# Moving four stages of a software pipeline within its period: a four-layer convolution network on one core

## The chip, the cores and the metric

The kernel runs on one core of a Trainium2 chip. The metric is the device time of one execution in microseconds (us). A core has TensorE (PE, with its weight loads shown as PEld), VectorE (DVE), ScalarE (ACT), GpSimd (POOL) and SyncE (SP, which here only issues DMAs). Each engine works through its own list of instructions, and semaphores order them between engines.

## The reference

The input x is 16 images of 64 x 64 pixels with 256 channels in float32. Four layers follow each other; each adds its result to x, and each works on a group norm (32 groups, over pixels and the group's channels) of its input:

- Layer 0: for each pixel the nearest of 1024 code vectors is found, and that vector is the result: `argmin(|x|^2 + |e|^2 - 2 x.e)`, then a gather.
- Layer 1: attention within each row of 64 pixels, `f = x Wf + bf`, `g = x Wg + bg`, `h = x Wh + bh`, `sigmoid(f g^T) h`.
- Layer 2: three projections of each pixel to a number, x0, x1 and x2. For every pair of the 4096 pixels n, m of an image `sim = x0[n] * x1[m]`, a softmax over n, `feats[m] = sum over n of x2[n] * softmax`, and the result is `sigmoid(feats[m]) * x`. These are 4096 x 4096 exponentials per image.
- Layer 3: linear attention with 4 heads of 32: softmax of q over the head's channels and of k over the pixels, a context matrix k v^T, its product with q, an output projection and a layer norm.

All arithmetic that matters for time is in float32.

## The kernel before

**Tiling.** A batch is one image: 4096 tokens, in 8 chunks of 512 tokens (4 tiles of 128). A chunk with its 256 channels on 2 x 128 partitions is a tile of 512 KB, and between stages it goes to DRAM and back. Each layer is cut into stages, and each stage is a Python generator that issues some instructions and then yields a number, the plan's measure of what it has issued:

- `stats0` (L287) loads a batch and takes its group-norm statistics.
- `search`, `stage1` (L303), is layer 0: the distances in `pd` (L377), VectorE's maximum (L384) and index search (L389) per tile of 128 tokens, 32 tiles per batch, the gather through POOL (L390).
- `layer1` (L416): `attend` and `mix` per chunk; `ph` and `po` are its large products, its result is added in L511. Search and layer 1 share two wide PSUM buffers (`wide`, L71).
- `rows`, `rows2` (L540): loads the 8 chunks again (`xr`), computes x0, x1, x2 in `pr` (L565), brings them to DRAM and, transposed, to `x01` (L575). `spread_rows` (L582) loads one row of 2048 numbers to all partitions.
- `exps`, `stage2` (L592): layer 2's exponentials, 64 pairs per batch of an exponential on ScalarE (L617) and a product with sum on VectorE (L620). The exponent's offset `nmax` comes from the extremes of x0 over all pixels (L598 to L604), which needs a reduction over partitions on POOL (L601). Its `nmax` tile has one buffer.
- `gate`, `gate2` (L653): per chunk the gate's row is loaded to all partitions (`gb`, L667), ScalarE makes `u` from it twice (L674), VectorE multiplies (L675) and takes statistics, and the chunk is stored (L681). `gb` has one buffer, `u2` two.
- `layer3`, `stage3` (L689): a first pass over the chunks for keys, queries, values and the context (L731 to L791), and a second for the output (`form`, `variance`, `po`, `pxo`, `y`).

**Order.** The instructions are traced in the order of a plan at the end of the kernel. Its unit is a period: the search of batch b lies at b to b + 1. `task` (L880) gives every stage of every batch a start, not before its predecessor's end plus a lag and not before the same stage of the batch before has ended, and a length. A heap then takes the generator that is next in plan time, lets it issue until its next yield, and moves it on by `length * step / total`. So the plan sets no time on the chip; it sets which instruction stands before which in each engine's list and in each queue. Work under `high_priority` may go ahead of it, and a DMA whose buffer is free may be issued ahead of an earlier one that waits. Six or so stages of as many batches lie in one period, in the steady part each once:

| stage of batch | search b | stats0 b+1 | layer1 b-1 | rows b-1 | exps b-2 | gate b-2 | layer3 b-3 |
|---|---|---|---|---|---|---|---|
| plan, from the period's start | 0 to 1 | 0.30 to 0.80 | 0.06 to 0.76 | 0.79 to 0.89 | -0.07 to 0.93 | 0.99 to 1.79 | -0.17 to 0.83 |

(The gate that starts at 0.99 runs into the next period, as do exps and layer 3. The gate and layer 3 have fewer units than their `total`, so that their last yields lie at some 0.88 of their lengths.) The first batches have a shorter layer 1 and the last ones shorter stages, by the constants of L33 to L38 and the lines of the loop (L886 to L898). In the last batch the exponentials are made in 8 parts, with the gate's chunks behind them.

Of the kernel before, what the change touches and what calls it, by code (L numbers as in the profile page):

```python
# [9 lines left out]
F32 = mybir.dt.float32  # L10
# [3 lines left out]
ALU = mybir.AluOpType  # L14
AX = mybir.AxisListType
# [14 lines left out]
HEADS = 4  # L30
DH = 32
URGENT = 3000
LAG1, LEN1 = 0.06, 0.7  # L33
LAGR = 0.03
LAG2 = 0.17
LAG3, LENG = 0.06, 0.8
LAG4 = 0.04
LEN3 = {0: 0.4, 1: 0.33, 2: 0.37}  # L38

# [2 lines left out]
def kernel(  # L42
# [497 lines left out]
    def rows2(b):  # L540
        tag = f"r2_{b}"
        scale, nmean, _ = norm2[b]
        with tc.high_priority(offset=URGENT):
            pb = bank(f"pbr_{tag}")
            for k in range(NK):
                nc.scalar.activation(
                    wrow_n[:, k, :].rearrange("p (j n) -> p j n", n=32)[:, :, 0:3],
                    wrow_raw[:, k : k + 1, 0:3].to_broadcast([P, 4, 3]), AF.Copy, scale=scale[:, k : k + 1],
                )
            for k in range(NK):  # L550
                nc.tensor.matmul(
                    pb[:, 0:1], lhsT=wrow_n[:, k, :], rhs=nmean[:, k : k + 1], start=(k == 0), stop=(k == NK - 1)
                )
            brow_n = small.tile([P, 1], F32, tag="brow_n", name=f"brow_{tag}")
            nc.scalar.activation(brow_n, pb[:, 0:1], AF.Identity, bias=brow)
        x01 = small.tile([P, NT, 2], F32, tag="x01", name=f"x01_{tag}", bufs=2)
        rd = dram.tile([3, 2, 4, CW], F32, tag="rows", name=f"rows_{tag}", bufs=3)
        for h in range(2):
            pr = bank(f"pr_{tag}_{h}")
            for j in range(4):  # L560
                xt = xb.tile([P, NK, CW], F32, tag="xb", name=f"xr_{tag}_{h}_{j}")
                nc.sync.dma_start(out=xt, in_=x2_d[b][4 * h + j])
                part = slice(32 * j, 32 * j + 32)
                for k in range(NK):
                    nc.tensor.matmul(  # L565
                        pr[part, :], lhsT=wrow_n[:, k, part], rhs=xt[:, k, :], start=(k == 0), stop=(k == NK - 1)
                    )
            rows = s1p.tile([P, CW], F32, tag="t4", name=f"rows_{tag}_{h}", bufs=5)
            nc.scalar.activation(rows, pr, AF.Identity, bias=brow_n)
            for n in range(3):  # L570
                nc.scalar.dma_start(out=rd[n, h], in_=rows[n : n + 97 : 32, :])
            pt = bank(f"prt_{tag}_{h}")
            for t in range(CH):
                nc.tensor.transpose(pt[:, t * P : (t + 1) * P], rows[:, t * P : (t + 1) * P], ident)
            nc.vector.tensor_copy(  # L575
                x01[:, 16 * h : 16 * h + 16, :].rearrange("p (j t) n -> p j t n", t=CH),
                pt.rearrange("p (t j n) -> p j t n", j=4, n=32)[:, :, :, 0:2],
            )
            yield 4
        rows_d[b] = x01, rd, [spread_rows(rd, b, 0)]  # L580

    def spread_rows(rd, b, h):  # L582

# [8 lines left out]
    def stage2(b, parts=1):  # L592

        tag = f"s2_{b}"
        x01, rd, halves = rows_d.pop(b)

        ext = small.tile([P, 2], F32, tag="ext", name=f"ext_{tag}", bufs=1)
        nc.vector.tensor_reduce(ext[:, 0:1], x01[:, :, 0], AX.X, ALU.max)  # L598
        nc.vector.tensor_reduce(ext[:, 1:2], x01[:, :, 0], AX.X, ALU.min, negate=True)
        ab = small.tile([P, 2], F32, tag="ab", name=f"ab_{tag}", bufs=1)  # L600
        nc.gpsimd.partition_all_reduce(ab, ext, P, bass_isa.ReduceOp.max)  # L601
        nmax = small.tile([P, NT], F32, tag="nmax", name=f"nmax_{tag}", bufs=1)
        nc.vector.tensor_scalar(nmax, x01[:, :, 1], ab[:, 0:1], -1.0, ALU.mult, ALU.mult)
        nc.vector.scalar_tensor_tensor(nmax, x01[:, :, 1], ab[:, 1:2], nmax, op0=ALU.mult, op1=ALU.min)  # L604
        den = small.tile([P, 2, NT], F32, tag="den", name=f"den_{tag}", bufs=1)
        num = small.tile([P, 2, NT], F32, tag="num", name=f"num_{tag}", bufs=1)
        halves.append(spread_rows(rd, b, 1))
        gd = dram.tile([NT, P], F32, tag="gate", name=f"gd_{tag}")
        gates_d[b] = gd
        yield 2  # L610
        rest = gate2(b) if parts > 1 else None
        for part in range(parts):
            those = range(part * NT // parts, (part + 1) * NT // parts)
            for h, (x0b, x2b) in enumerate(halves):
                for T in those:
                    ex = s2p.tile([P, TOK // 2], F32, tag="ex", name=f"ex_{tag}_{h}_{T}", bufs=3)
                    nc.scalar.activation(  # L617
                        ex, x0b, AF.Exp, bias=nmax[:, T : T + 1], scale=x01[:, T, 1:2], accum_out=den[:, h, T : T + 1]
                    )
                    nc.vector.tensor_tensor_reduce(  # L620
                        out=ex, in0=ex, in1=x2b, scale=1.0, scalar=0.0, op0=ALU.mult, op1=ALU.add,
                        accum_out=num[:, h, T : T + 1],
                    )
                    yield 2.4
            n = len(those)
            cols = slice(those[0], those[0] + n)
            gate = small.tile([P, NT], F32, tag="gate", name=f"gate_{tag}_{part}", bufs=1)[:, 0:n]
            nc.vector.tensor_tensor(gate, den[:, 0, cols], den[:, 1, cols], ALU.add)
            nc.vector.reciprocal(gate, gate)
            nsum = small.tile([P, NT], F32, tag="nsum", name=f"nsum_{tag}_{part}", bufs=1)[:, 0:n]  # L630
            nc.vector.tensor_tensor(nsum, num[:, 0, cols], num[:, 1, cols], ALU.add)
            nc.vector.tensor_tensor(gate, gate, nsum, ALU.mult)
            nc.scalar.activation(gate, gate, AF.Exp, scale=-1.0)
            nc.vector.tensor_scalar(gate, gate, 1.0, None, ALU.add)
            nc.vector.reciprocal(gate, gate)
            yield 1
            pg = bank(f"pgt_{tag}_{part}")
            nc.tensor.transpose(pg[:n, :P], gate, ident)
            grow = small.tile([NT, P], F32, tag="grow", name=f"grow_{tag}_{part}", bufs=1)
            nc.scalar.copy(grow[:n, :], pg[:n, :P])  # L640
            nc.scalar.dma_start(out=gd[cols, :], in_=grow[:n, :])
            yield 1
            if rest is not None and part >= parts // 2 - 1:
                yield next(rest)
                if part > parts // 2:
                    yield next(rest)
        if rest is not None:
            yield from rest
# [4 lines left out]
    def gate2(b):  # L653
# [9 lines left out]
        for ch in range(NCHUNK):  # L663
            xt = xg.tile([P, NK, CW], F32, tag="xg", name=f"xg_{tag}_{ch}")
            nc.sync.dma_start(out=xt, in_=x2[ch])
            gb = s3p.tile([P, CW], F32, tag="gb", name=f"gb_{tag}_{ch}", bufs=1)
            nc.sync.dma_start(  # L667
                out=gb,
                in_=gd[ch * CH : (ch + 1) * CH, :].rearrange("t p -> (t p)").rearrange("(o n) -> o n", o=1)
                .to_broadcast([P, CW]),  # L670
            )
            for k in range(NK):
                u = s3p.tile([P, CW], F32, tag="u2", name=f"u_{tag}_{ch}_{k}")
                nc.scalar.activation(u, gb, AF.Identity, bias=one, scale=scale[:, k : k + 1])  # L674
                nc.vector.scalar_tensor_tensor(  # L675
                    xt[:, k, :], xt[:, k, :], nmean[:, k : k + 1], u, op0=ALU.add, op1=ALU.mult
                )
            chunk_stats(st3, xt, ch)
            yield 4
            d = dram.tile([P, NK, CW], F32, tag=f"x3_{ch}", name=f"x3_{tag}_{ch}", bufs=3)  # L680
            nc.sync.dma_start(out=d, in_=xt)  # L681
            x3.append(d)
# [203 lines left out]
    for b in range(nb):  # L886
        left = nb - 1 - b
        if b > 0:
            tasks.append((b - 0.7, 0.5, stats0(b), 14))
        task("search", b, 1.0, stage1(b), 160)  # L890
        end = task("layer1", b + 1 + LAG1, (LEN1 if b else 0.2) if left else 0.35, layer1(b), 88)
        task("rows", end + LAGR, 0.1, rows2(b), 8)
        if left:
            end = task("exps", end + LAG2, 1.0, stage2(b), 160)
            end = task("gate", end + LAG3, 0.15 if left == 1 else LENG, gate2(b), 36)
        else:
            end = task("exps", end + LAG2, 0.65, stage2(b, NCHUNK), 200)
        task("layer3", end + LAG4, LEN3.get(left, 1.0), stage3(b), 160)  # L898
    for _ in stats0(0):
        pass  # L900
    queue = [(start, n) for n, (start, _, _, _) in enumerate(tasks)]
# [43 lines left out]
```

## Time and profile before

| what | value |
|---|---|
| median of three runs | 5923.42 us (5917.82 to 5939.97) |
| the profiled execution | 5928.44 us, its span 5926.7 us |
| granted TensorE clock, mean | 0.941 |
| busy | PE 90%, DVE 86%, ACT 77%, POOL 33% |
| exponentials on VectorE, L620 | 2350.7 us, 1024 of 2302 ns |
| exponentials on ScalarE, L617 | 2137.8 us, 1024 of 2088 ns |
| distances on TensorE, L377 | 2022.2 us, 4096 of 623 ns |
| maximum and index search on VectorE, L384 and L389 | 622.2 and 624.1 us, 512 each |
| DMA | 1059.47 MB, mean 179 GB/s |

The span runs from the first to the last instruction. A row of a window has the window, its length, then for PE, PEld, DVE, ACT and POOL the busy time and the number of instructions, then the granted TensorE clock, the mean busy share of the DMA engines and GB/s. A row of waits has the engine and line that waited, what it waited for, and the microseconds in total, the times and the longest. An engine's wait counts only where the engine was idle.

### The profile page before, as it was taken

Reading aid. Unit: us, or ns where it says so; the run is one execution under the profiler, and the core shown is the slowest. Engines: PE = TensorE matmul, PEld = TensorE weight load, DVE = VectorE, ACT = ScalarE, POOL = GpSimd, SP = SyncE. Lnnn points to the kernel's source line nnn. Section 1 sums busy time; section 2 is a strip of 40 time slices with the busy share of each in tenths; the row PEclk is TensorE's granted clock in tenths of the full one; section 3 lists DMA queues with packets and bytes.
Section 4 is the critical chain, followed back from the end, with each engine's and each line's share of the span. In section 5 each row is a group of like instructions: output and inputs, shape, how many; then the busy total and the mean of one; then the engine's idle time right before and its main releaser. Section 6 shows DMA issues by size and latency. Waiting matters only on the chain.

```text
span 5926.7 us, 79561 instructions
## 1 busy us (share of the span) xinstructions
PE 5337.4 (90%) x28239; PEld 3211.1 (54%) x28239; DVE 5121.1 (86%) x7282; ACT 4570.8 (77%) x6754; POOL 1939.4 (33%) x1314
## 2 busy tenths in 40 slices
PE   8968899889999999998989999898999989997777
PEld 3524465545656565564656556565555646564555
DVE  6499798989989898898989889898998989888882
ACT  4377687878778787887879788797878878787873
POOL 3122233224233332433334233342424333231331
PEclk9989999989999898999999899999999999998899
DMA  6544745555656656565665656656565664644543
GB/s 186 162 124 124 225 137 177 184 184 162 207 168 192 197 151 202 184 207 181 184 205 167 194 183 188 206 174 204 164 210 164 202 204 147 209 158 173 184 158 116
DMA packets 521380, 1059.47 MB, mean 179 GB/s; under 512 B 52504, under 2 KB 266392, under 8 KB 512792
## 3 DMA queue, kind: packets, MB, share of 16 engines
q1 hardware_dynamic: 406288, 885.11, 44.7%
q0 software_dynamic: 73728, 67.14, 7.9%
q10 hardware_dynamic: 40968, 102.13, 4.5%
q8 instruction: 224, 3.67, 0.3%
q14 instruction: 172, 1.41, 0.1%
HBM read 751.18 MB, written 303.04 MB: 178 GB/s over the span
## 4 chain that ended last, share of the span: by engine, by line
PE 48%; DVE 16%; ACT 12%; DMA 7%; issue 6%; POOL 4%; ACTq 0%; SPq 0%; POOLq 0%; DVEq 0%
PE pd_s L377 15%; DVE ex_s L620 6%; ACT ex_s L617 5%; PE ph_l L468 5%; PE pqv_s L759 3%; PE po_s L854 3%; PE pk_s L737 3%; PE po_l L506 2%; PE pr_r L565 2%; DMA xr_r<-x_l 2%; DVE i_s L389 2%; POOL qv_s L779 2%; PE pvr_s L834 1%; PE pz_s L826 1%; DMA qo_s<-qd_s 1%
## 5 line engine op out<-in xcount | busy, mean ns | idle before, releaser
L620 DVE CUSTOM_DVE_ANT_0 ex_s<-ex_s,x2b 128x2048 f32<-128x2048 f32 x1024 | 2350.7, 2302 | 46.2 <-ACT ex_s L617 44.9
L617 ACT ACTIVATE ex_s<-x0b,nmax_s,x_r 128x2048 f32<-128x2048 f32 x1024 | 2137.8, 2088 | 66.4 <-DVE num_s L620 60.3
L377 PE MATMUL pd_s<-e,xn_s 128*128 128x512 f32 x4096 | 2022.2, 623 | 43.5 <-DVE m L384 40.8
L390 POOL DMA_INDIRECT xc_s<-in_emb_rows,i_s x512 | 1058.1, 2067 | 2063.9 <-DVE i_s L389 1466.8
L377 PEld LDWEIGHTS pd_s<-e,xn_s 128*128 128x128 f32 x4096 | 754.4, 197 | 764.9 <-issue 669.1
L384 DVE CUSTOM_DVE_ANT_0 nd_s<-pd_s,nn_s 128x1024 f32<-128x1024 f32 x512 | 622.2, 1215 | 174.4 <-ACT nn_s L372 82.1
L389 DVE FIND_INDEX8 i_s<-m,nd_s 128x8 uint32<-128x1024 f32 x512 | 624.1, 1219 | 0.0
L372 ACT ACTIVATE nn_s<-ne,nx_s 128x1024 f32<-128x1024 f32 x512 | 583.2, 1141 | 21.5 <-DVE nx_s L343 15.7
L468 PE MATMUL ph_l<-wh_l,xt_l 128*128 128x256 f32 x2048 | 525.5, 393 | 28.3 <-DVE m L384 16.5
L759 PE MATMUL pqv_s<-wqv_s,xk_s 128*128 128x256 f32 x2048 | 494.6, 382 | 0.0
L759 PEld LDWEIGHTS pqv_s<-wqv_s,xk_s 128*128 128x128 f32 x2048 | 390.9, 192 | 127.5 <-issue 65.5
L468 PEld LDWEIGHTS ph_l<-wh_l,xt_l 128*128 128x128 f32 x2048 | 380.9, 193 | 143.8 <-issue 57.5
L837 POOL TENSOR_TENSOR lrs_s<-lrs_s,mhalf 128x4 f32<-128x4 f32 x128 | 183.0, 1429 | 749.3 <-ACT lrs_s L836 710.5
L857 ACT ACTIVATE y_s<-po_s,lrs_s 128x256 f32<-128x256 f32 x512 | 237.1, 469 | 214.8 <-PE po_s L854 166.2
L854 PE MATMUL po_s<-wctx_s,qo_s 128*128 128x256 f32 x1024 | 336.0, 415 | 32.3 <-ACT y_s L857 31.1
L506 PE MATMUL po_l<-at_l,h_l 64*128 64x64 f32 x4096 | 318.5, 297 | 46.2 <-DVE xt_l L511 42.7
L506 PEld LDWEIGHTS po_l<-at_l,h_l 64*128 64x128 f32 x4096 | 286.5, 206 | 108.5 <-DVE xt_l L511 48.9
L779 POOL TENSOR_TENSOR qv_s<-qv_s,qm_s 128x512 f32<-128x512 f32 x128 | 232.7, 1818 | 312.3 <-DVE qm_s L778 181.7
L728 POOL TENSOR_TENSOR qv_s<-qv_s,qd_s 128x512 f32<-128x512 f32 x128 | 199.8, 1561 | 304.6 <-DVE qd_s L727 252.9
L865 DVE TENSOR_TENSOR y_s<-pxo_s,y_s 128x512 f32<-128x512 f32 x256 | 175.2, 686 | 125.0 <-ACT y_s L857 123.2
L854 PEld LDWEIGHTS po_s<-wctx_s,qo_s 128*128 128x128 f32 x1024 | 178.2, 198 | 172.5 <-ACT y_s L857 84.7
L737 PE MATMUL pk_s<-xk_s,wk_s 128*128 128x512 f32 x512 | 269.6, 650 | 0.0
(195 smaller groups left out, 7519.8 us busy)
## 6 DMA issues: line engine op xcount, KB each, us to landing
xs_s<-in_xT SPq DMA_DIRECT2D x128, 512.0 KB
xt_s<-in_xT SPq DMA_DIRECT2D x128, 512.0 KB
xc_s<-in_x SPq DMA_DIRECT2D x128, 512.0 KB
x_s<-xt_s ACTq DMA_DIRECT2D x128, 512.0 KB
xt_l<-x_s SPq DMA_DIRECT2D x128, 512.0 KB
x_l<-xt_l SPq DMA_DIRECT2D x128, 512.0 KB
xr_r<-x_l SPq DMA_DIRECT2D x128, 512.0 KB
xg_g<-x_l SPq DMA_DIRECT2D x128, 512.0 KB
```

Of the source, the lines that this page charges most:

```text
L372: nc.scalar.activation(nn, ne2, AF.Identity, bias=nx2[ch][:, t : t + 1])
L377: nc.tensor.matmul(pd[:, cols], lhsT=xn[ch][:, k, t * P : (t + 1) * P], rhs=e2[:, k, cols], start=(k == 0), stop=(k == NK - 1),)
L384: nc.vector.tensor_tensor_reduce(out=nd, in0=pd, in1=nn, scale=1.0, scalar=-3.0e38, op0=ALU.add, op1=ALU.max, accum_out=m8[:, 0:1],)
L389: nc.vector.max_index(i8, m8, nd)
L390: nc.gpsimd.indirect_dma_start(out=xc[ch][:, t, :], out_offset=None, in_=emb_rows, in_offset=bass.IndirectOffsetOnAxis(ap=i8[:, 0:1], axis=0),
L468: nc.tensor.matmul(ph[:, t, :], lhsT=X[:, k, t * P : (t + 1) * P], rhs=wh_n[:, k, :], start=(t % 2 == 0 and k == 0), stop=False, skip_grou ...
L506: nc.tensor.matmul(po[:, r, k * CH + t, :], lhsT=h[rows, t, k * P : (k + 1) * P], rhs=at[rows, t, :], start=True, stop=True,)
L617: nc.scalar.activation(ex, x0b, AF.Exp, bias=nmax[:, T : T + 1], scale=x01[:, T, 1:2], accum_out=den[:, h, T : T + 1])
L620: nc.vector.tensor_tensor_reduce(out=ex, in0=ex, in1=x2b, scale=1.0, scalar=0.0, op0=ALU.mult, op1=ALU.add, accum_out=num[:, h, T : T + 1],)
L737: nc.tensor.matmul(pk, lhsT=wk_n[:, k, :], rhs=xt[:, k, :], start=(k == 0), stop=(k == NK - 1))
L759: nc.tensor.matmul(pqv[:, j, :], lhsT=xt[:, k, t * P : (t + 1) * P], rhs=wqv_n[:, k, :], start=(j == 0 and k == 0), stop=False, skip_group ...
L854: nc.tensor.matmul(po[:, j, :], lhsT=qT[:, t * P : (t + 1) * P], rhs=wctx[:, 1, :], start=True, stop=True)
```

## The change

The plan's constants change, the maxima move, and two small tiles trade buffers:

- Layer 1 takes 0.5 of a period where it took 0.7 (0.2, 0.3 and 0.4 for the first three batches, where it was 0.2 for the first and 0.7 for the others; 0.3 for the last, where it was 0.35). Rows, exps, gate and layer 3 follow its end, so in the steady part they start 0.2 earlier in the period; layer 3, which follows the shorter gate, 0.23 earlier.
- The gate takes 0.77 (0.8) and layer 3 0.9 (1.0) of a period. `stats0` starts 0.5 of a period before its search, over 0.45, where it started 0.7 before it, over 0.5.
- The extremes of x0, the reduction over partitions and `nmax` are issued at the end of `rows2`, not at the start of `stage2`; `nmax` has two buffers. The same seven lines, with one buffer for `nmax`, are gone from the start of `stage2`; the diff shows them once. `rows2` has one yield more, and its total goes from 8 to 9.
- `gb` has two buffers. `u` for the first half of the channels has one buffer; for the second half ScalarE writes it over `gb`.

```diff
-LAG1, LEN1 = 0.06, 0.7
+LAG1, LEN1 = 0.06, 0.5
 LAGR = 0.03
 LAG2 = 0.17
-LAG3, LENG = 0.06, 0.8
+LAG3, LENG = 0.06, 0.77
...
-        rows_d[b] = x01, rd, [spread_rows(rd, b, 0)]
+
+        ext = small.tile([P, 2], F32, tag="ext", name=f"ext_{tag}", bufs=1)
+        nc.vector.tensor_reduce(ext[:, 0:1], x01[:, :, 0], AX.X, ALU.max)
+        nc.vector.tensor_reduce(ext[:, 1:2], x01[:, :, 0], AX.X, ALU.min, negate=True)
+        ab = small.tile([P, 2], F32, tag="ab", name=f"ab_{tag}", bufs=1)
+        nc.gpsimd.partition_all_reduce(ab, ext, P, bass_isa.ReduceOp.max)
+        nmax = small.tile([P, NT], F32, tag="nmax", name=f"nmax_{tag}", bufs=2)
+        nc.vector.tensor_scalar(nmax, x01[:, :, 1], ab[:, 0:1], -1.0, ALU.mult, ALU.mult)
+        nc.vector.scalar_tensor_tensor(nmax, x01[:, :, 1], ab[:, 1:2], nmax, op0=ALU.mult, op1=ALU.min)
+        rows_d[b] = x01, nmax, rd, [spread_rows(rd, b, 0)]
+        yield 1
...
-        x01, rd, halves = rows_d.pop(b)
+        x01, nmax, rd, halves = rows_d.pop(b)
...
-            gb = s3p.tile([P, CW], F32, tag="gb", name=f"gb_{tag}_{ch}", bufs=1)
+            gb = s3p.tile([P, CW], F32, tag="gb", name=f"gb_{tag}_{ch}", bufs=2)
...
-                u = s3p.tile([P, CW], F32, tag="u2", name=f"u_{tag}_{ch}_{k}")
+                u = s3p.tile([P, CW], F32, tag="u2", name=f"u_{tag}_{ch}_{k}", bufs=1) if k == 0 else gb
...
-            tasks.append((b - 0.7, 0.5, stats0(b), 14))
+            tasks.append((b - 0.5, 0.45, stats0(b), 14))
         task("search", b, 1.0, stage1(b), 160)
-        end = task("layer1", b + 1 + LAG1, (LEN1 if b else 0.2) if left else 0.35, layer1(b), 88)
-        task("rows", end + LAGR, 0.1, rows2(b), 8)
+        end = task("layer1", b + 1 + LAG1, min(LEN1, 0.2 + 0.1 * b) if left else 0.3, layer1(b), 88)
+        task("rows", end + LAGR, 0.1, rows2(b), 9)
...
-        task("layer3", end + LAG4, LEN3.get(left, 1.0), stage3(b), 160)
+        task("layer3", end + LAG4, LEN3.get(left, 0.9), stage3(b), 160)
```

More of the change, by code (lines that the diff above doesn't have):

```diff
@@ L594, in stage2 @@
         tag = f"s2_{b}"
-        x01, rd, halves = rows_d.pop(b)
[L597 to L604, printed above, removed]
+        x01, nmax, rd, halves = rows_d.pop(b)
         den = small.tile([P, 2, NT], F32, tag="den", name=f"den_{tag}", bufs=1)
```

## The prediction

> **What bounds the kernel now.** I read the page's busy shares first, then cut the span into periods (the starts of the 16 batches' first index searches, L389), then one period into stretches of the plan, then the waits.
>
> The page, engines:
>
> ```profile
> PE 5337.4 (90%) x28239; PEld 3211.1 (54%) x28239; DVE 5121.1 (86%) x7282; ACT 4570.8 (77%) x6754; POOL 1939.4 (33%) x1314
> ```
>
> Two engines are near full. VectorE's 5121.1 us are 320.1 us a batch. Busy time by window (stretch, its length, then PE, PEld, DVE, ACT, POOL), for ramp-up, the third period and the sixth:
>
> ```profile
> 169.10:480.50 311.40, 241.89 (x1269) 124.81 (x1267) 221.53 (x303) 193.75 (x260) 70.81 (x42) 0.91 0.44 137
> 480.50:727.80 247.30, 217.03 (x1200) 115.76 (x1199) 206.94 (x309) 165.23 (x232) 66.93 (x40) 0.94 0.64 197
> ...
> 1370.60:1722.80 352.20, 329.42 (x1765) 199.84 (x1765) 319.25 (x452) 284.40 (x422) 123.69 (x81) 0.95 0.60 188
> ```
>
> From 1371 us on the periods last 347 to 358 us (the last search, at the ramp-down's edge, 325), with VectorE idle some 32 us of each. The time after the last search:
>
> ```profile
> 5219.50:5460.00 240.50, 198.15 (x1263) 134.30 (x1262) 209.58 (x259) 200.26 (x310) 52.56 (x43) 0.90 0.49 167
> 5460.00:5700.00 240.00, 177.19 (x784) 122.66 (x783) 214.98 (x312) 192.89 (x306) 88.35 (x66) 0.87 0.50 170
> 5700.00:5926.70 226.70, 178.17 (x835) 123.00 (x833) 101.48 (x169) 103.62 (x207) 45.13 (x55) 0.90 0.41 135
> ```
>
> VectorE is 88% busy up to 5700, then half idle while the last gate and layer 3 finish. One steady period (batch 8's search), cut at search tiles 9 and 23, which stand at 0.29 and 0.74 of the plan's period:
>
> ```profile
> 2436.60:2524.70 88.10, 86.46 (x502) 53.31 (x501) 81.95 (x118) 81.27 (x118) 39.59 (x25) 1.00 0.48 140
> 2524.70:2695.70 171.00, 158.08 (x956) 102.09 (x955) 159.93 (x225) 136.74 (x208) 50.69 (x32) 0.97 0.68 211
> 2695.70:2783.70 88.00, 76.64 (x311) 39.53 (x311) 74.56 (x114) 66.58 (x98) 35.63 (x25) 0.98 0.64 202
> ```
>
> Over nine steady periods these average 88.7, 173.7 and 89.9 us for 0.2625, 0.45 and 0.2875 of the plan: 338, 386 and 313 us per unit. The middle, where layers 1 and 3, gate and stats0 lie on each other, is slow; the end, with rows, leaves VectorE 15% idle.
>
> **The skill.** The Trainium skill, Perfetto Trace Analysis, Identifying the Most-Contended Engine, says TensorE's busy share is a poor measure; the trace agrees: a pd matmul lasts 623 ns by its row, but eight follow each other in 3.43 us (429 ns each) on the chain. The same page, Optimization Strategy, advises interleaving regimes with different bounds; that fits the three rates above. TensorE: Matmul & The Clock Gate, on the 16× 32×32 array, calls VectorE's and ScalarE's queues strict FIFO; the trace agrees: VectorE's copy of the rows (L575) waited 110.8 us for TensorE, with all later work behind it. DMA: Bandwidth & Descriptors, Issuing engines are not separate DMA queues, says that SP's and ScalarE's transfers share the same 16 DMA engines; so the second gb buffer adds no bandwidth, only an earlier start, and the DMA share of 0.48 to 0.68 in the period above leaves room for that.
>
> **Work and plan.** VectorE per batch, each instruction counted until the next starts: search 86 us, exps 145, layer 1 19, gate 21, stats0 10, layer 3 35, rest 4: 320. TensorE at dense pace (unbroken runs, lower quartile): search 126 (pd 256 x 0.429 = 110), layer 1 59 (ph 128 x 0.216 = 28, po 256 x 0.06 = 15), rows 16, layer 3 99 (pqv 128 x 0.216 = 28, pk and po 14 each), rest 3: 303.
>
> Before, within the period: layer 1 at 0.06-0.75, stats0 0.30-0.73, rows 0.79-0.89, layer 3 0.83-1.72 (it yields 142 of 160), gate 0.99-1.69. Work divided by length gives VectorE/TensorE per unit: 327/324 up to 0.30, 350/324 to 0.72, then 231 to 300 against 126 to 398.
>
> After: layer 1 0.06-0.55, stats0 0.50-0.89, rows 0.59-0.69, layer 3 0.60-1.40, gate 0.79-1.47. That gives P (0.06-0.40, all overlap) 343/370; Q (0.40-0.59) 284/221; R (rows, 0.59-0.69) 300/410; S (0.69-1.06) 311/250.
>
> **Steady period.** The middle stretch ran at 386 against its larger load of 350 (1.10), the first at 338 against 327 (1.03), the last, summed over its finer pieces, at 1.065. I take 1.03 for Q and S, where one engine has room, 1.065 for R, and 1.067 for P, between the two: 370 x 1.067 = 395. So 0.34 x 395 = 134.3; 0.19 x 293 = 55.7; 0.10 x 437 = 43.7; 0.37 x 320 = 118.5; sum 352.2. The steady period stays: VectorE becomes evener, TensorE more uneven. Bounds, P at 1.03 to 1.11 and the others at 1.03 to 1.06: 347 to 361.
>
> **Pipeline depth.** Exps and all behind them come 0.2 period earlier, so the plan ends at 17.82 instead of 18.02. Behind the last search lies less VectorE work: 0.2 x 145 exps + 0.31 x 21 gate + 0.31 x 35 layer 3 = 46 us; at 0.88 busy, -53 us. But this work is done earlier. The third period takes 0.4 exps more (58 us), the next two 0.1 less each, and layer 3 of batch 1 comes 0.4 earlier (15 us). The third period has 247.3 - 206.9 = 40 us of VectorE idle, but TensorE is 88% busy there, so little fills: I charge +40. Net -13 (0 to -30). The half-idle last 227 us keep their lengths of plan and stay.
>
> **gb and u2.** 128 gate chunks. ScalarE waited 32.4 us for gb in all (10 times), none of it among the steady waits; at 569 to 615 and near 5770 the chain runs from one gb load to the next (4.66, 6.03, 3.50 us). Two buffers save about half of that: -15 (0 to -30). In the steady part the wait is SP's:
>
> ```profile
> SPq L667 <- ACT u_g L674: 293.5, 51, 14.1
> ```
>
> That is 33 us a period with the queue's loads behind it, but chunk ch+1's gb stands just before chunk ch's store, which waits for the VectorE product that uses u, so the wait moves to L681, issued 1 to 4 us later in the gate chunks at 2798 to 2888. Zero there (-2 to +1 a period). A single u2 waits for a product one chunk old, 31 us before in the steady part and about 8 us in the densest gate (62 us for eight chunks): nothing; with chunks under 2 us it would cost one product, 0.8 us each.
>
> **Maxima.** The same instructions move: two reductions, one POOL all-reduce, two products, 0.2, 0.4 and 0.2 us by their rows. No DMA moves with them. Behind the products on VectorE stand search and exps; ScalarE's first exponential waits for them. Today they cost VectorE 6.3 us and ScalarE 4.2 us in all; their new place can add a wait of one POOL operation, 1.8 us (L779) per batch. Range -10 to +29, taken -4. The second nmax buffer is a small tile; no other stall hung on it.
>
> **Sum.** Profiled execution: span 5926.7, time 5928.4. -13 - 15 - 4 + 0 = -32: 5896. The median is 5 us under the profiled run, so about 5890.
>
> **Rivals.**
> (1) Evenness pays. P runs at the first stretch's 1.03 (381) and the others as taken, with rows hidden under layer 3 (41): 129.5 + 55.7 + 41 + 118.5 = 345; eleven periods x -7 = -80, with the -32: 5810. For it: the last stretch's idle VectorE. Against it: one wait stays with rows,
>
> ```profile
> DVE x_r L575 <- PE prt_r L574: 58.3, 17, 6.2
> ```
>
> 6.5 us a period in nine steady ones, from TensorE's chain of xr loads, pr and transposes.
> (2) TensorE becomes the bound where layers 1 and 3 meet (P). In 0.34 of the period it must do 126 us, even with no stall, against a period's even share of 120. At 1.11, 411 per unit, and S at 1.06, the period is 361: +9 x 11 - 32 = +67, 5990. Layer 1's wide PSUM buffers rotate with search's, already 63 us of TensorE waits in nine periods (po, ph, pd on VectorE). It turns the sign from 354.9 a period (+32 in all), and is slower by over 0.5% from 357.6. Against it: batch 0's layer 1 ran in 68 us, so its chain of loads and stores is no limit at 22 us a chunk.
> (3) Nothing measurable: the ramp takes back all that the tail gives and the gb waits are hidden by others: 5920.
>
> **Numbers.** Forecast 0.42 (own range 5850 to 5925), (1) 0.16, (2) 0.32, (3) 0.10. About 0.5% (30 us) is what a measurement here tells from no change: faster is below 5894. The forecast gives 0.26 of faster and 0.16 of same, (1) all faster, (3) 0.08 same and 0.02 slower, (2) slower: 0.42, 0.24, 0.34. The range 5805 to 6005 leaves half of (1)'s and a third of (2)'s far sides out.
>
> **What would show it.** Right: steady periods of 349 to 355 us; VectorE's idle in them moved from the rows to P and R; after the last search about 650 us, not 707; the third period near 290; hardly any wait for gb. Rival 2: more waits of VectorE on pd, po and y in P, and TensorE solid there. I am wrong if the steady period moves by over 5 us either way, which eleven periods turn into 55.

## The result, and the profile after

The changed kernel takes 6068.93 us (median of four, 6064.79 to 6071.41) against 5927.76: 1.0236 times the time before, with a 95% interval of 1.0215 to 1.0258. It is slower, by 2.4%, and outside the range given. The profiled execution took 6067.74 us, its span is 6066.0 us, 139.3 more than before. The page's engines:

```profile
PE 5362.7 (88%) x28239; PEld 3225.8 (53%) x28239; DVE 5163.1 (85%) x7282; ACT 4582.7 (76%) x6754; POOL 1942.0 (32%) x1314
```

The instructions are the same in number. VectorE's busy time grew by 42 us (19 us each in the exponentials' products and in the gate's, whose instructions take longer), its idle time by 97. Cut at the starts of the searches (L389), as before, the 139 us lie here:

| part of the span | before | after | difference |
|---|---|---|---|
| to the third search | 480.5 | 481.0 | 0 |
| third period | 247.3 | 300.3 | +53 |
| fourth | 324.6 | 356.3 | +32 |
| fifth | 318.2 | 346.0 | +28 |
| sixth to fifteenth | 3523 (352.3 each) | 3569 (356.9 each) | +45 |
| sixteenth, the last search | 326 | 347 | +21 |
| behind the last search | 707 | 667 | -40 |

Busy time by window in the fourth and fifth period of the kernel before:

```profile
727.80:1052.40 324.60, 301.98 (x1602) 183.30 (x1602) 287.76 (x401) 262.75 (x380) 111.31 (x77) 0.94 0.50 156
1052.40:1370.60 318.20, 281.33 (x1465) 159.18 (x1464) 293.56 (x404) 254.56 (x355) 89.98 (x56) 0.91 0.58 180
```

and in the second to fifth of the changed kernel:

```profile
171.90:480.80 308.90, 244.31 (x1267) 125.97 (x1266) 220.94 (x300) 193.82 (x259) 74.54 (x42) 0.87 0.44 133
480.80:781.00 300.20, 232.99 (x1199) 120.54 (x1199) 256.56 (x349) 219.85 (x283) 70.41 (x40) 0.87 0.55 164
781.00:1137.70 356.70, 319.70 (x1688) 191.33 (x1687) 298.51 (x431) 265.55 (x395) 126.36 (x80) 0.94 0.57 174
1137.70:1484.00 346.30, 312.49 (x1668) 188.19 (x1669) 294.05 (x417) 260.04 (x385) 116.30 (x78) 0.94 0.55 169
```

In the third period VectorE has 50 us more work than before (206.9) in 53 us more time, while TensorE's matmuls are as many as before. In the fifth it is the other way: VectorE's 294 us are as before (293.6), and TensorE has some 200 matmuls more (1465 before), of layer 3 of the second batch, batch 1. (In the table of the order the layer 3 at -0.17 to 0.83 is that of batch b-4; that of batch b-3 starts at 0.83, so batch 1's stood at 4.83 and now stands at 4.40.) The fourth period has 86 matmuls and 11 us of VectorE's work more: layer 3 of the first batch, now in 0.9 of a period, has 500 of its matmuls there, where it had 416. As an estimate at the dense pace of the prediction, TensorE's work in the three periods went from 202, 279 and 250 us to 202, 293 and 287; VectorE's busy time went from 207, 288 and 294 to 257, 299 and 294.

After the last search:

```profile
5399.20:5640.00 240.80, 202.10 (x1248) 140.02 (x1248) 199.97 (x255) 189.12 (x297) 57.93 (x42) 0.87 0.48 159
5640.00:5880.00 240.00, 181.61 (x744) 121.81 (x745) 208.50 (x302) 191.84 (x301) 75.96 (x57) 0.81 0.50 164
5880.00:6066.00 186.00, 146.29 (x708) 100.97 (x708) 65.89 (x118) 70.00 (x157) 33.78 (x46) 0.92 0.41 138
```

VectorE has 474 us of work here, not 526; it is 85% busy in the first two windows, where it was 88%.

A steady period (batch 8's search) at tiles 2, 12, 18, 22 and 34, which stand at 0.075, 0.39, 0.575, 0.70 and 1.075 of the plan, so that the first window is about the prediction's P:

```profile
2568.90:2694.90 126.00, 125.41 (x839) 82.58 (x838) 110.57 (x146) 107.09 (x163) 37.62 (x19) 0.97 0.61 185
2694.90:2755.60 60.70, 54.73 (x306) 31.18 (x305) 56.06 (x74) 43.34 (x63) 13.39 (x11) 0.92 0.57 175
2755.60:2798.90 43.30, 39.27 (x154) 19.69 (x153) 36.27 (x59) 30.51 (x45) 12.21 (x7) 1.00 0.83 280
2798.90:2925.50 126.60, 108.32 (x495) 67.01 (x494) 120.08 (x179) 106.78 (x158) 59.77 (x45) 0.96 0.54 159
```

TensorE is solid in the first window, at VectorE's cost: 110.6 of 126 us. Over nine periods these four run at 393, 323, 364 and 340 us per unit of plan; cut at the same tiles, the kernel before runs at 356, 392, 416 and 308. Waits of VectorE between 1723 and 4894 us, first in the kernel before

```profile
DVE nd_s L384 <- PE pd_s L377: 2.5, 2, 1.2
```

then in the changed one:

```profile
DVE nd_s L384 <- PE pd_s L377: 53.9, 44, 3.3
...
DVE nmax_r L587 <- POOL ab_r L585: 30.9, 9, 6.2
DVE x_r L575 <- PE prt_r L574: 21.9, 16, 3.8
```

VectorE now waits for the distances and for the maxima, and less for the rows (58.3 before). Waits of the SP queue over the span, two of the kernel before

```profile
SPq L667 <- ACT u_g L674: 433.3, 86, 14.1
...
SPq L681 <- DVE xg_g L675: 164.6, 92, 7.9
```

and one of the changed kernel:

```profile
SPq L682 <- DVE xg_g L676: 544.8, 110, 21.9
```

SP's wait for a free `gb` (433.3 us) is gone, and its wait at the store has grown by 380.

### The profile page after: what moved, and what is told of

Its sections match the earlier page's. It is cut to its first block, busy times and chain, and to the rows that moved or that the text cites. A ratio compares the mean times of both kernels' runs of the same rounds, so it can differ in the third digit from the quotient of the medians.

```text
span 6066.0 us, 79469 instructions
## 1 busy us (share of the span) xinstructions
PE 5362.7 (88%) x28239; PEld 3225.8 (53%) x28239; DVE 5163.1 (85%) x7282; ACT 4582.7 (76%) x6754; POOL 1942.0 (32%) x1314
## 4 chain that ended last, share of the span: by engine, by line
PE 48%; DVE 17%; ACT 9%; issue 6%; DMA 4%; POOL 4%; ACTq 0%; POOLq 0%; DVEq 0%; SPq 0%
PE pd_s L377 15%; DVE ex_s L621 6%; PE ph_l L468 5%; ACT ex_s L618 4%; PE po_s L855 4%; PE po_l L506 3%; DVE i_s L389 3%; PE pqv_s L760 2%; DMA qo_s<-qd_s 2%; PE pz_s L827 2%; PE pk_s L738 2%; DVE nd_s L384 2%; PE pfg_l L457 2%; PE pxo_s L860 2%; PE pvr_s L835 2%
## 5 line engine op out<-in xcount | busy, mean ns | idle before, releaser
L618 ACT ACTIVATE ex_s<-x0b,nmax_r,x_r 128x2048 f32<-128x2048 f32 x1024 | 2139.3, 2090 | 100.7 <-DVE num_s L621 59.8
L377 PE MATMUL pd_s<-e,xn_s 128*128 128x512 f32 x4096 | 2062.7, 634 | 126.6 <-DVE m L384 114.2
L389 DVE FIND_INDEX8 i_s<-m,nd_s 128x8 uint32<-128x1024 f32 x512 | 623.2, 1217 | 0.0
L838 POOL TENSOR_TENSOR lrs_s<-lrs_s,mhalf 128x4 f32<-128x4 f32 x128 | 205.3, 1604 | 693.7 <-ACT lrs_s L837 664.9
L729 POOL TENSOR_TENSOR qv_s<-qv_s,qd_s 128x512 f32<-128x512 f32 x128 | 214.5, 1676 | 355.3 <-DVE qd_s L728 160.9
L506 PE MATMUL po_l<-at_l,h_l 64*128 64x64 f32 x4096 | 294.1, 288 | 31.7 <-DVE nx_s L343 31.7
L506 PEld LDWEIGHTS po_l<-at_l,h_l 64*128 64x128 f32 x4096 | 267.8, 199 | 93.1 <-issue 66.0
```

The source lines that it names most:

```text
L377: nc.tensor.matmul(pd[:, cols], lhsT=xn[ch][:, k, t * P : (t + 1) * P], rhs=e2[:, k, cols], start=(k == 0), stop=(k == NK - 1),)
L389: nc.vector.max_index(i8, m8, nd)
L506: nc.tensor.matmul(po[:, r, k * CH + t, :], lhsT=h[rows, t, k * P : (k + 1) * P], rhs=at[rows, t, :], start=True, stop=True,)
L618: nc.scalar.activation(ex, x0b, AF.Exp, bias=nmax[:, T : T + 1], scale=x01[:, T, 1:2], accum_out=den[:, h, T : T + 1])
```

## The experiments

The text takes the runs in the order in which they were made. The columns come from one execution of each kernel, the one with the trace: start of the sixth search (the ramp's length), mean of the ten periods from there, the last search, and the time behind it. Executions of one kernel differ too: those of the kernel before lie between 5908 and 5962 us, some 3 us a period.

| kernel | ratio to before (95%) | sixth search | period | last search | behind it |
|---|---|---|---|---|---|
| before | 1 | 1371 | 352.3 | 326 | 707 |
| the change | 1.0236 (1.0215 to 1.0258) | 1484 | 356.9 | 347 | 667 |
| before_plan | 1.0278 (1.0257 to 1.0299) | 1477 | 361.1 | 345 | 677 |
| after_max_old | 1.0298 (1.0279 to 1.0318) | 1468 | 360.7 | 348 | 665 |
| before_max_new | 1.0116 (1.0087 to 1.0145) | 1374 | 358.9 | 328 | 707 |
| before_gb | 1.0026 (1.0015 to 1.0037) | 1371 | 352.1 | 331 | 718 |
| layer1_half | 1.0217 (1.0183 to 1.0252) | 1361 | 365.0 | 341 | 715 |
| plan_old_depth | 1.0219 (1.0195 to 1.0243) | 1383 | 362.2 | 325 | 727 |
| stats_late | 1.0367 (1.0343 to 1.0391) | 1391 | 374.0 | 335 | 701 |
| layer1_long | 1.0203 (1.0176 to 1.0230) | 1363 | 360.9 | 341 | 741 |
| lag1_tiny | 1.0114 (1.0085 to 1.0143) | 1361 | 359.6 | 337 | 701 |
| lag3_tiny | 1.0146 (1.0124 to 1.0168) | 1383 | 359.4 | 331 | 717 |
| stats_tiny | 0.9926 (0.9899 to 0.9953) | 1371 | 345.1 | 326 | 720 |
| stats_tiny2 | 0.9988 (0.9973 to 1.0003) | 1374 | 350.5 | 333 | 713 |
| after_lag1_tiny | 1.0200 (1.0179 to 1.0221) | 1462 | 358.0 | 335 | 661 |
| after_lag3_tiny | 1.0180 (1.0136 to 1.0224) | 1475 | 354.8 | 332 | 673 |
| after_stats_tiny | 1.0221 (1.0177 to 1.0264) | 1484 | 357.0 | 341 | 666 |
| after_l3_late | 1.0195 (1.0156 to 1.0234) | 1445 | 359.0 | 339 | 666 |

**The parts alone.** Theory M: the maxima cost in their new place. In the steady part of the two traces POOL's reduction starts 6.6 to 10.2 us after POOL's previous instruction; before, POOL stood waiting for the extremes in that time, and now a gather mostly ends just then. Theory P: the plan alone costs. The edits were the parts of the diff shown above, each put into the kernel before; in after_max_old the maxima alone were put back:

```diff
 # after_max_old: the seven lines from rows2 back to the start of stage2, nmax with one buffer
-        task("rows", end + LAGR, 0.1, rows2(b), 9)
+        task("rows", end + LAGR, 0.1, rows2(b), 8)
```

> The kernel before with only the plan's constants changed, maxima and gate buffers as before. Theory M: 6010 to 6035, ramp some 100 us later at the start of the sixth search, steady period within 2 us of before. Theory P: 6060 to 6075, steady period 4 us longer.

> The changed kernel with the maxima put back to the start of the exponentials' stage; plan and gate buffers stay changed. Theory M (the maxima's new place costs by the set-up of POOL's reduction, which an earlier wait hid before): 6068 less some 45, 6010 to 6035. Theory P (the plan alone costs, the maxima's waits only take the place of others): 6060 to 6075.

> The kernel before with only the maxima moved behind the rows. Theory M: 5955 to 5985, with VectorE's wait for the reduction at 2 to 6 us a batch. Theory P: 5920 to 5935. If the set-up is exposed only where a gather stands just before the reduction, as in the new plan: 5920 to 5935 and no such gather in the trace.

> The kernel before with only the two gb buffers and the single u2. Both theories, and the forecast's -15: 5905 to 5930; the wait of ScalarE for gb falls from 32 us to below 20.

Measured: 6098.62, 6106.11, 5998.89 and 5942.95 us. The plan alone costs more than the whole change, and in the new plan the maxima's move saves 37 us where in the old one it costs 70. M falls as the cause of the loss, since the plan alone, without M's wait, costs as much. Each of these edits also gives the lists another order, and one part's price depends on the rest. In before_max_new VectorE hardly waits for the reduction (8.6 us over the span), and its period is 6.6 us longer all the same. The gb edit takes ScalarE's wait for gb from 32.4 to 23.8 us, not below 20, and gains nothing. SP in before_gb:

```profile
SPq L681 <- DVE xg_g L675: 432.8, 95, 17.2
```

Before, SP waited 433.3 us for a free gb at the load and 164.6 at the store. The first is gone, the second has grown by 268; the rest of SP's waiting went without a gain in time. In before_plan and in after_max_old two transfers come late, in the change they do not. The waits of before_plan from 1850 to 4850 us:

```profile
ACT xn_s L322 <- DMA xt_s<-in_xT: 40.0, 8, 6.0
DVE st_s L249 <- DMA xs_s<-in_xT: 33.7, 14, 4.1
```

In after_max_old these are 38.9 and 33.9 us, in the change the first does not occur and the second is 3.2. The 74 us in some eight periods are 9 a period, more than the 4 us a period between before_plan and the change; that they are its cause was not tested by itself.

**Which part of the plan.** Theory C: the denser layer 1, meeting layer 3, makes TensorE the bound (the prediction's rival 2). Theory S: the earlier place of what follows costs.

```diff
 # layer1_half
-LAG1, LEN1 = 0.06, 0.7
+LAG1, LEN1 = 0.06, 0.5
...
-            end = task("exps", end + LAG2, 1.0, stage2(b), 160)
+            end = task("exps", end + LAG2 + (0.2 if b else 0.0), 1.0, stage2(b), 160)
 # plan_old_depth: layer1_half, and the change's lines for stats0, LENG and layer 3's 0.9
 # stats_late
-            tasks.append((b - 0.7, 0.5, stats0(b), 14))
+            tasks.append((b - 0.5, 0.45, stats0(b), 14))
 # layer1_long
-LAG1, LEN1 = 0.06, 0.7
+LAG1, LEN1 = 0.06, 0.8
```

> The kernel before with layer 1 (and the rows behind it) in half a period, but exponentials, gate and layer 3 kept at their old places by a longer lag. Theory C (the denser layer 1, where it meets layer 3, makes TensorE the bound): steady period 357 to 363 instead of 352, 5980 to 6040. Theory S (what costs is the earlier place of exponentials and layer 3, not layer 1's length): steady period 347 to 354, 5880 to 5950. Both: sixth search starts within 20 us of before (1371), 700 to 715 us after the last search.

> The new plan (short layer 1, late statistics, short gate and layer 3), but exponentials and what follows kept 0.2 of a period later, where they were. If the loss in the ramp comes from the earlier exponentials and layer 3: sixth search at 1360 to 1400 and not 1477, 700 to 715 us after the last search. Theory C: steady period 357 to 363, 5980 to 6040; theory S: 347 to 354, 5880 to 5950.

> The kernel before with only the statistics moved from 0.30-0.80 to 0.50-0.95 of the period. If VectorE's load in the densest stretch counts: steady period 347 to 351, 5870 to 5915. If it is hidden: 5920 to 5940.

> The kernel before with layer 1 in 0.8 of a period where it took 0.7, all behind it 0.1 later: the change's direction turned round. Theory C: steady period 346 to 351; ramp 0 to 50 us shorter, end 15 us longer, 5850 to 5920. Theory S, or a steady period that cannot be bettered: 5925 to 5960.

Measured: 6067.1, 6063.33, 6154.44 and 6057.15 us. The ramp came out clearly. plan_old_depth starts its sixth search at 1383, not 1477 as before_plan does, and takes 727 us behind the last search (more than was expected), not 677: 94 us of the ramp and 50 of the end belong to the earlier exponentials and what follows them, net 44. (It also keeps the old lengths of layer 1 in the first and last batches, which were not tried alone.) Its third and fourth period:

```profile
481.80:727.60 245.80, 214.43 (x1201) 113.54 (x1200) 199.22 (x299) 161.18 (x226) 67.88 (x40) 0.94 0.65 197
727.60:1075.10 347.50, 317.46 (x1686) 193.35 (x1687) 308.13 (x430) 278.35 (x408) 118.08 (x80) 0.95 0.54 163
```

The third is as short as before. The fourth is not (324.6 before, 348.8 in before_plan): it holds the matmuls that layer 3's shorter length brings into it, so most of its growth is not from the earlier exponentials. The steady period fits neither theory. layer1_half seems to speak for C, but with a longer layer 1 the kernel is as slow as with a shorter one, the statistics alone cost most of all, and plan_old_depth, which holds that same move, is 12 us a period better than stats_late. Every step away from the old plan costs 9 to 22 us a period, in whatever direction.

**Shifts that change no load.** So the next kernels move one stage, or one and those that follow it, by 0.005 of a period, 1.8 us. A draw, below, is the order that one such plan happens to give.

```diff
 # lag1_tiny (after_lag1_tiny: the same in the changed kernel)
-LAG1, LEN1 = 0.06, 0.7
+LAG1, LEN1 = 0.065, 0.7
 # lag3_tiny
-LAG3, LENG = 0.06, 0.8
+LAG3, LENG = 0.065, 0.8
 # stats_tiny
-            tasks.append((b - 0.7, 0.5, stats0(b), 14))
+            tasks.append((b - 0.695, 0.5, stats0(b), 14))
```

> The kernel before with layer 1, and all that follows it, 0.005 of a period (1.8 us) later. No engine's load in any stretch changes. Theory F (the steady period hangs on the fine order that the plan happens to give, and the old plan's is a good draw): steady period 355 to 368, 5960 to 6090. Theory L (loads of stretches and the depth decide): 351 to 354, 5920 to 5945.

> The kernel before with gate and layer 3 alone 0.005 of a period later. Theory F: steady period more than 2 us from 352, more likely longer: 5950 to 6080. Theory L: 5920 to 5945.

> The kernel before with the statistics of the next batch alone 0.005 of a period later; moved by 0.2 they cost 3.7%. Theory F: a period that has nothing to do with the size of the shift, 352 to 372, 5925 to 6150. Theory L: 5920 to 5945.

> The changed kernel with layer 1, and all that follows it, 0.005 of a period later. Theory F: the steady period moves by more than 2 us from 357, either way, 6000 to 6150. Theory L: within 10 us of 6069.

Measured: 5999.15, 6018.34, 5877.76 and 6043.09 us. Theory F holds for the old layout, though stats_tiny falls below the range that it gave: its period goes from 345 to 360 us for nothing but another order of the same instructions. In the new layout the first shift fits neither theory: the period moves by 1.1 us only, the time by 26. The engines' lines of the pages of stats_tiny

```profile
PE 5291.4 (90%) x28239; PEld 3178.2 (54%) x28239; DVE 5119.5 (87%) x7282; ACT 4567.3 (78%) x6754; POOL 1925.4 (33%) x1314
```

and of lag3_tiny

```profile
PE 5386.2 (89%) x28239; PEld 3224.3 (54%) x28239; DVE 5148.2 (85%) x7282; ACT 4573.8 (76%) x6754; POOL 2035.2 (34%) x1314
```

show VectorE's work within 29 us of each other, in spans of 5868.5 and 6025.6 us. What differs are many small waits. VectorE's longest ones between 1723 and 4894 us, first in stats_tiny

```profile
DVE x_r L575 <- PE prt_r L574: 53.8, 17, 5.4
DVE y_s L865 <- ACT y_s L857: 43.1, 38, 3.4
DVE nd_s L384 <- ACT nn_s L372: 29.5, 30, 1.6
DVE ex_s L620 <- ACT ex_s L617: 26.7, 30, 1.2
```

then in lag3_tiny:

```profile
DVE y_s L865 <- ACT y_s L857: 85.7, 30, 8.3
DVE x_r L575 <- PE prt_r L574: 61.0, 15, 6.5
DVE ex_s L620 <- ACT ex_s L617: 51.8, 36, 4.4
```

In the second, layer 3's addition and the exponentials wait up to 8.3 and 4.4 us at a time, in the first 3.4 and 1.2. Per steady period VectorE is idle for 28 us in stats_tiny, 35 before and 39 in lag3_tiny. stats_tiny is faster than both the kernel before and the changed one.

The granted TensorE clock is a rival that no run takes alone. Over 56 executions of the kernel before, a hundredth less of it goes with some 43 us more, as cause or as result. stats_tiny has 0.945 and lag3_tiny 0.935 where the kernel before has 0.940, so by that slope some 20 us of each one's difference go with the clock, and as much of the change's (0.936). But lag1_tiny and plan_old_depth are slower by 69 and 131 us at 0.942: the clock alone does not make the scatter.

**Open then: is the new layout's 357 a draw, and why did the ramp cost so much.**

```diff
 # after_lag3_tiny, after_stats_tiny: the shifts above, in the changed kernel (0.065; b - 0.495)
 # stats_tiny2: stats0 at b - 0.69 in the kernel before
 # after_l3_late: in the changed kernel
-        task("layer3", end + LAG4, LEN3.get(left, 0.9), stage3(b), 160)
+        task("layer3", end + LAG4 + (0.43 if b == 1 else 0.0), LEN3.get(left, 0.9), stage3(b), 160)
```

> The changed kernel with gate and layer 3 alone 0.005 of a period later. If the new layout itself costs: steady period 356 to 362, 6040 to 6120. If its 357 is a draw like the old layout's: anywhere from 346 to 362, 5960 to 6120. Sixth search at 1460 to 1485 either way.

> The changed kernel with the statistics alone 0.005 of a period later, the shift that gave the old layout 345 us a period. New layout costs: 355 to 362, 6040 to 6120. A draw: 346 to 362, 5960 to 6120.

> The kernel before with the statistics alone 0.01 of a period later; at 0.005 the steady period fell to 345. If the gain belongs to later statistics: 340 to 347, 5840 to 5890. If it is a draw: 346 to 362, 5880 to 6030.

> The changed kernel with layer 3 of batch 1 alone 0.43 of a period later, where it stood before; the later ones catch up by batch 4. If the fifth period is long for TensorE's 37 us of layer 3 in it: 346 falls to 315 to 325, and the work comes back in the next three periods at less than its price, 6040 to 6065. If it is long for the shallower pipeline as such: 340 to 350, 6060 to 6100.

Measured: 6038.84, 6069.32, 5924.17 and 6046.04 us. Four draws about the new layout have periods of 354.8 to 358.0, mean 356.7; five about the old one 345.1 to 359.6, mean 353.4. The means differ by 3.3 us, with the old ones scattered by 14.5. after_lag3_tiny lies just below the ranges for a layout that costs, after_stats_tiny within those of both. Whether the new layout costs anything in the steady part stays open; none of its four draws is as good as the 345, 350 or 352 of the old. stats_tiny2 shows that later statistics are no gain by themselves either.

after_l3_late shows the ramp's second term. Its fourth to sixth period:

```profile
778.80:1132.50 353.70, 315.58 (x1687) 188.98 (x1685) 298.17 (x430) 264.88 (x394) 126.38 (x80) 0.96 0.57 175
1132.50:1444.60 312.10, 264.49 (x1371) 145.33 (x1372) 268.89 (x372) 232.63 (x320) 80.17 (x51) 0.91 0.55 165
1444.60:1814.80 370.20, 343.42 (x1846) 206.31 (x1846) 331.95 (x465) 291.18 (x440) 130.80 (x91) 0.98 0.58 181
```

With layer 3 of batch 1 back where it stood, the fifth period takes 312 us, not 346 (332 to 350 in the four draws). So layer 3's place is the cause; both engines lose work there, VectorE 25 us, and that TensorE's is what counts rests on the kernel before, whose fifth period is short with the same work of VectorE. 12 us come back in the sixth and about as much in the seventh, where VectorE and TensorE work at once. In the end the time is 23 us under the changed kernel's, within the range given, but no further than shifts of 1.8 us take it.

## Why the prediction was wrong

The forecast's sum was -32; the profile shows +139. The prediction's sign of being wrong, a steady period moved by over 5 us, did not come (4.6). By its own steps:

- **Pipeline depth (-13): this step failed.** The end behind the last search was priced at -53 for 46 us of VectorE work; 52 us left it, and it shortened by 40, since VectorE's share there fell from 0.88 to 0.85 in the first windows. The ramp was priced at +40, VectorE's added exponentials in the third period alone; that period gave +53. The step took "layer 3 of batch 1 comes 0.4 earlier (15 us)" by its VectorE work and priced it at nothing. TensorE's work of layer 3, by estimate some 37 us more in the fifth period and, by layer 3's shorter length in batch 0, 14 in the fourth, was left out, and these periods grew by 28 and 32. The two engines' added work falls in different periods, so the prices add up: +113 in the ramp, +73 with the end, by place over half of the loss. before_plan against plan_old_depth gives the earlier exponentials and what follows them +94 and -50, +44 in all, where -13 was forecast; after_l3_late shows layer 3's part of it, 34 us in the fifth period, of which some 24 come back later. The fourth period's growth stays in both, and its cause was not tested by itself.
- **Steady period (unchanged, bounds 347 to 361).** The size held its bounds: 356.9. P ran at 393 where 395 was forecast, Q at 323 against 293, and from 0.575 to 1.075 the rate was 346 against some 345. Within that last stretch two misses cancel, by luck: up to 0.70, with R, 364 against some 410, behind it 340 against some 323. TensorE solid in P with VectorE waiting for pd is rival 2's sign (the waits for y, which it named too, fell from 50.3 to 32.9 us), and before_plan has its very period, 361. But the step took 352 as what the old layout gives, with factors read from its three stretches to the third digit. Shifts of 1.8 us move that period to between 345 and 360; the factors were those of one draw. The +45 is no more than such shifts give, and of the last search's +21 some 8 are left between the means of the two layouts' draws. Whether these 66 us have another cause than the draw stays open.
- **gb and u2 (-15).** Right that SP's wait moves to the store, for the greater part of it; the gain did not come: +0.26% alone (0.15 to 0.37), with 8.6 us less waiting for gb on ScalarE.
- **Maxima (-4, range -10 to +29).** Alone +70, in the new plan -37. The wait at the reduction, 42.4 us over the span where 6.3 stood before, is real and was named, but taken too small: the step read 0.37 us from the reduction's row, not the time before it. The +70 is no more than shifts of 1.8 us give in the old layout and the -37 little more than they give in the new one (-30), and no cause is shown for either.
- **Rival 2 at 0.32** had the sign, by a mechanism that the runs leave open (the steady period); the turning point it gave, 354.9 a period, was of no use with the ramp mispriced. No case spoke of the order of the lists, and the range was narrow for it: 0.005 of a period alone makes -0.7% to +1.5%.

## What to carry to other kernels

In a kernel with two engines at nine tenths, whose order comes from a plan with small buffers, measure first what shifts without meaning do; a change smaller than that scatter cannot be forecast from loads, and a single order of it proves nothing of its idea. Price a ramp per period and per engine: work that is brought forward for two engines into different periods costs both prices, though it leaves one place at the end.

## What the runs showed of the hardware

The reduction over partitions on POOL reads 0.37 us in its row, but in the steady part of the kernel before, the changed one and before_max_new it started 6.3 to 10.2 us after POOL's previous instruction. POOL in the changed kernel:

```profile
3501.32 1.58 POOL L390 DMA_INDIRECT xc_s<-in_emb_rows,i_s  x1 [8.17 <-DVE qd_s L727]
3510.69 0.37 POOL L585 PARTITION_ALL_REDUCE ab_r<-ext_r  x1 [7.79 <-issue]
```

The extremes were ready at 3501.3 and the result came at 3511.1; VectorE and ScalarE, at the product and the first exponential, waited 2.9 and 2.3 us of it. It does not take a gather: at 1727.2 us the reduction stands 10.2 us behind a small product of layer 3 (L749), with the extremes ready before that product ended. In the kernel before POOL's 8 us are put down to the extremes:

```profile
3084.51 0.37 POOL L601 PARTITION_ALL_REDUCE ab_s<-ext_s  x1 [8.06 <-DVE ext_s L599]
```

There the extremes came 0.14 us before the start. So idle time put down to a late input can hide idle time that would be there without it; what POOL does in it is not shown by these traces.
